# Layer 1's first pass moved ahead of its flag's branch, with chunks loaded or kept under attention and stores issued by GpSimd

## The chip, the cores and the metric

One Trainium2 chip, and of it one core. The time is the device time of one execution in microseconds (us), as the median over runs. A core has five engines that work at the same time, each with its own queue in program order: PE (TensorE, matmuls; its weight loads are listed as PEld), DVE (VectorE), ACT (ScalarE), POOL (GpSimd), and SP (SyncE, which here issues DMA transfers). ACT and POOL can issue DMA transfers too, in queues of their own. Sixteen DMA engines move the data of all queues.

## The reference

Four layers work on x of 256 x 256 x 128 floats, each as x = x + layer(group_norm(x)). The layer that is changed here is the second, called layer 1; layer 0 is the attention whose end comes just before it.

```python
# layer 0: gated triangle attention (4 heads of 32), with pair bias
x = x + _L0_conv_ref(_gn(x), ...)
# layer 1: gated triangle product over 16 channels
def _L1_conv_ref(x, Wa1, ba1, Wa2, ba2, Wb1, bb1, Wb2, bb2, ln2_g, ln2_b, Wg, bg, Wz, bz):
    a = jax.nn.sigmoid((x @ Wa1 + ba1) * (x @ Wa2 + ba2))
    b = jax.nn.sigmoid((x @ Wb1 + bb1) * (x @ Wb2 + bb2))
    g = jax.nn.sigmoid(x @ Wg + bg)
    z = jnp.einsum('bikc,bkjc->bijc', a, b)
    return g * (_ln(z, ln2_g, ln2_b) @ Wz + bz)
x = x + _L1_conv_ref(_gn(x), ...)
# layers 2 and 3 follow: a triangle product over 128 channels, and a layer of small convolutions
```

`_gn` subtracts mean and divides by deviation over groups of 4 channels, taken over the whole image. So layer 1's weights can be folded only when the statistics of all of x1 (the output of layer 0) are known.

## The kernel before

The image is held channel first: x1T in DRAM is 128 channels (partitions) x 65536 tokens. Layers work through it in chunks of SC = 2048 tokens (32 chunks of 1 MB); attention works in groups of GT = 1024 tokens (64 groups of four rows), so that chunk s is groups 2s and 2s + 1.

*Attention (the loop over j, 0 to 2 NG + 4, NG = 64).* Everything inside stands in an order written by hand (`tc.manual_schedule()`). Step j computes scores and weights for two rows, attends the rows of the step before, and finishes older groups: `gate` multiplies by the gate and sends the reciprocal of the softmax sum through DRAM (rz, rb) by SP, `divide` applies it (POOL; for the last group DVE, L730), `output` adds the projection to x (L740), and `close` takes `bn_stats` (L744) and stores the group to x1T (L747; SP, for the last two groups ACT). At j = 2 NG + 2 DVE aggregates the statistics of all groups but the last (`gn_part`, L181), between the divide and the last output. The attention tiles lie in pools on the right side of SBUF (`att_sb`, tags x, xn, rs, qk, vg; `tri_pool` with tri_raw) and on the left (`p2e`, `p2u`).

*The flag.* When attention is done, 13 slots of one chunk each are made on the left, and SP issues the loads of the first 8 chunks (`load1`, L851). The statistics are merged to mv1, and a flag says whether all are finite (L861 to L866). All engines read the flag (L867) and branch on it (L868): if it is set, `general_attention` does layer 0 again in a slower, safe manner. In the runs here it is not set, and the body is jumped over. Behind the branch come the group norm's factors (`gn_groups`) and the folded weights v1, v2, wgf with their offsets (L887 to L902).

*First pass (L921 to L941, by hand).* For each of the 32 chunks PE makes two products (16 matmuls of 32 columns, L927), ACT adds an offset (L936), DVE multiplies (L937), ACT takes the sigmoid one chunk later (L913), and SP stores the result of 256 KB to abD (L918), one to two chunks later still. On SP the store of a chunk stands behind the load of a later chunk into the slot that was just read. The result tile p3_ab has 12 buffers.

*z stage and second pass.* SP loads a and b of two channels at a time from abD (`load_z`), PE multiplies them, and the normalised z goes to znD. The second pass (L1017 to L1097) goes over the chunks in the list `order`, beginning with the 13 that are still in slots: PE and ACT make the gate, PE the product with z, DVE and POOL add to x, SP stores x2T and reloads a slot four steps after its chunk was done. POOL issues the loads of z (L1024). At the end POOL also issues the first four loads of layer 2 (L1160), and SP three more, into tiles that overlie the slots.

Outside the parts in a hand-written order, the framework chooses the order of instructions on each engine; nothing is moved across a branch. Names in the trace drop the stage prefix's number: p3_ab is `p_ab`, p4_z is `p_z`, the chunks are `x`.

Of the kernel before, what the change touches and what calls it, by code (L numbers as in the profile page):

```python
# [15 lines left out]
P = 128  # L16
N = 256
# [14 lines left out]
def kernel(ctx: ExitStack, tc: tile.TileContext, a: dict, out: bass.AP):  # L32
# [162 lines left out]
    def gn_groups(mv, name):  # L195

        with tc.tile_pool(name=name + "_ps", bufs=1, space=PSUM, reuse_waits="tile") as ps, tc.tile_pool(name=name + "_sb", bufs=1, reuse_waits="tile") as sb:
# [4 lines left out]
            d = sb.tile([P, 1], F32, name=name + "_d")  # L202
# [4 lines left out]
            sd = sb.tile([P, 1], F32, name=name + "_sd")  # L207
# [37 lines left out]
    raw = tri_pool.tile([P, NH + 2, 2, N], F32, name="tri_raw")  # L245
# [351 lines left out]

    stats1 = new_stats("stats1")
    rzD = dram.tile([N // 4, 16, N], F32, name="rzD")
    NG = N // G  # L600
    with tc.tile_pool(name="p2e", bufs=6, reuse_waits="tile") as eb, tc.tile_pool(name="p2c", bufs=1, reuse_waits="tile") as cs:
        with att_scope, tc.tile_pool(name="p2u", bufs=2, reuse_waits="tile") as sb, tc.tile_pool(name="p2S", bufs=2, space=PSUM, reuse_waits="tile") as psS, tc.tile_pool(name="p2z", bufs=1, space=PSUM, reuse_waits="tile") as psZ, tc.tile_pool(name="p2M", bufs=3, space=PSUM, reuse_waits="tile") as psM, ExitStack() as by_hand:
            rows = {}
# [119 lines left out]
            def divide(g):  # L723
                t = groups[g]
                if g == NG - 1:

                    rb = psS.tile([P, 2, 2, N], F32, name="p2_S")
                    for r in range(G):
                        nc.tensor.matmul(rb[:, r // 2, r % 2, :], lhsT=pick[:, r, :], rhs=t["rz"], start=True, stop=True)
                    nc.vector.tensor_tensor(t["u"], t["u"], rb.rearrange("p a b n -> p (a b n)"), ALU.mult)  # L730
                    return
# [10 lines left out]
            def close(g, c):  # L742
                x1 = groups[g]["x"]
                nc.vector.bn_stats(stats1[:, g * 2 + c, :], x1[:, c * CK : (c + 1) * CK])  # L744
                if c == 1:
                    queue = nc.sync if g < NG - 2 else nc.scalar
                    queue.dma_start(x1T[:, g * GT : (g + 1) * GT], x1)  # L747
                    del groups[g]
# [21 lines left out]
            for j in range(2 * NG + 5):  # L770
# [5 lines left out]
                if not 0 <= out[0] < NG:  # L776
                    out = None
                if j == 20:
# [34 lines left out]
                if back:  # L813
                    attend(2 * j - 4)
                    gate(2 * j - 4)
                if now:
# [17 lines left out]
                if j == 2 * NG + 2:  # L834
                    mv_first = gn_part(stats1, 0, 2 * NG - 2, "gn1_a")
# [7 lines left out]
    order1 = [b + h * NSC // 2 for b in range(NSC // 2) for h in range(2)]  # L843
    SLOTS, FIRST = 13, 8
    x1_scope = ExitStack()
    slots = [x1_scope.enter_context(tc.tile_pool(name=f"x1_{i}", bufs=1, reuse_waits="tile")) for i in range(SLOTS)]
    xs = {}

    def load1(s, slot):
        xs[s] = slots[slot].tile([P, SC], F32, name="x1", tag="x1")  # L850
        nc.sync.dma_start(xs[s], x1T[:, s * SC : (s + 1) * SC])  # L851

    for i in range(FIRST):
        load1(order1[i], i)


    mv1 = gn_merge(mv_first, gn_part(stats1, 2 * NG - 2, 2 * NG, "gn1_b"), 1.0 - 1.0 / NG, "gn1_mv")
    flag = const.tile([P, 1], mybir.dt.int32, name="flag")
    with tc.tile_pool(name="chk", bufs=1, reuse_waits="tile") as sb, tc.tile_pool(name="chkps", bufs=1, space=PSUM, reuse_waits="tile") as ps:
        ok = sb.tile([P, 2], F32, name="chk_ok")  # L860
        nc.vector.tensor_scalar(ok, mv1, 0.0, 0.0, ALU.mult, ALU.is_equal)  # L861
        pn = ps.tile([P, 2], F32, name="chk_n")
        nc.tensor.matmul(pn, lhsT=ones, rhs=ok, start=True, stop=True)
        bad = sb.tile([P, 2], F32, name="chk_bad")
        nc.vector.tensor_scalar(bad, pn, P - 0.5, None, ALU.is_lt)
        nc.vector.tensor_tensor(flag, bad[:, 0:1], bad[:, 1:2], ALU.max)  # L866
    again = nc.values_load(flag[0:1, 0:1], min_val=0, max_val=1)  # L867
    with tc.If(again > 0):  # L868
        general_attention(
            tc, dict(xT=xT, rsD=rsD, mbD=mbD, triD=triD, x1T=x1T),  # L870
            dict(wf=wf, wo=wo, b_g=b_g, b_o=b_o, cqkg=cqkg, cv=cv, mneg=mneg, ident=ident),
            dram, stats1,
        )
        nc.vector.bn_aggr(mv1, stats1.rearrange("p n s -> p (n s)"))
        for s in order1[:FIRST]:
            nc.sync.dma_start(xs[s], x1T[:, s * SC : (s + 1) * SC])

    m1, r1 = gn_groups(mv1, "gn1")
# [6 lines left out]
    with tc.tile_pool(name="f1ps", bufs=1, space=PSUM, reuse_waits="tile") as ps:  # L889
        for w, wf_, ub, vb, n in ((u1, v1, ub1, vb1, "1"), (u2, v2, ub2, vb2, "2")):  # L890
            nc.vector.tensor_scalar(wf_, w, r1, None, ALU.mult)
            pb = ps.tile([P, 1], F32, name="f1_u" + n)
            for q in range(4):
                nc.tensor.matmul(pb[32 * q : 32 * q + 32, :], lhsT=wf_, rhs=m1, start=True, stop=True)
            nc.vector.tensor_tensor(vb, ub, pb, ALU.subtract)
        nc.vector.tensor_scalar(wgf, wg1, r1, None, ALU.mult)
        pb = ps.tile([P, 1], F32, name="f1_g")
        nc.tensor.matmul(pb, lhsT=wgf, rhs=m1, start=True, stop=True)
        nc.vector.tensor_tensor(bgf, bg1, pb, ALU.subtract)

    c1neg = const.tile([P, 1], F32, name="c1neg")
    nc.vector.tensor_scalar(c1neg, mv1[:, 0:1], -1.0, None, ALU.mult)  # L902
# [1113 lines left out]
```

## Time and profile before

| | us |
|---|---|
| median of 3 runs (lowest, highest) | 3257.12 (3255.87, 3260.84) |
| the profiled execution's own time | 3257.65 |
| its span, first to last instruction | 3255.9 |
| PE busy | 3049.4 |
| DVE busy | 2265.3 |
| ACT busy | 2030.4 |
| POOL busy | 1722.0 |
| attention's last scores to first matmul of the first pass | 1442.25 to 1480.44 |
| first pass, first matmul to last sigmoid's start | 1480.44 to 1555.57 |
| first transpose of the z stage | 1565.71 |
| second pass, first product with z to last chunk's store issued | 1632.62 to 1790.73 |

The granted TensorE clock was 0.971 on average. Times in the text count from the start of the span of this one execution. In a line of instructions a bracket or a last column says how long the engine stood idle before, and what ended it ("<-").

### The profile page before, as it was taken

Reading aid. Unit: us, or ns where it says so; the run is one execution under the profiler, and the core shown is the slowest. Engines: PE = TensorE matmul, PEld = TensorE weight load, DVE = VectorE, ACT = ScalarE, POOL = GpSimd, SP = SyncE. Lnnn points to the kernel's source line nnn. Section 1 sums busy time; section 2 is a strip of 40 time slices with the busy share of each in tenths; the row PEclk is TensorE's granted clock in tenths of the full one; section 3 lists DMA queues with packets and bytes.
Section 4 is the critical chain, followed back from the end, with each engine's and each line's share of the span. In section 5 each row is a group of like instructions: output and inputs, shape, how many; then the busy total and the mean of one; then the engine's idle time right before and its main releaser. Section 6 shows DMA issues by size and latency. Waiting matters only on the chain. (4 is left out here: it accounts for less than half of the span.)

```text
span 3255.9 us, 51705 instructions
## 1 busy us (share of the span) xinstructions
PE 3049.4 (94%) x19908; PEld 1631.7 (50%) x19908; DVE 2265.3 (70%) x2623; ACT 2030.4 (62%) x2272; POOL 1722.0 (53%) x917
## 2 busy tenths in 40 slices
PE   5699999999999999987798899999999989969998
PEld 4535555555555555542533344444699933324444
DVE  5657888888888888883456455455455588858887
ACT  3577777777777777754477544444344457757776
POOL 4006777777777777760277000000255568848787
PEclk8899999999999999998999899999999999989999
DMA  9972333333333333349789577676799989976775
GB/s 376 394 297 95 117 119 107 115 119 108 114 120 109 113 119 110 113 146 398 220 307 412 213 295 300 235 272 247 274 352 351 338 326 388 387 273 196 234 231 154
DMA packets 291508, 748.27 MB, mean 230 GB/s; under 512 B 68473, under 2 KB 139019, under 8 KB 242459
## 3 DMA queue, kind: packets, MB, share of 16 engines
q1 hardware_dynamic: 282065, 731.02, 62.6%
q0 software_dynamic: 6064, 12.21, 1.1%
q8 instruction: 160, 2.62, 0.3%
q10 hardware_dynamic: 3128, 1.67, 0.2%
q14 instruction: 91, 0.75, 0.1%
HBM read 457.35 MB, written 287.45 MB: 229 GB/s over the span
## 5 line engine op out<-in xcount | busy, mean ns | idle before, releaser
L670 POOL TENSOR_TENSOR p_es<-p_e 128x1024 f32<-128x1024 f32 x256 | 603.5, 2368 | 319.4 <-DMA p_x<-xT 196.2
L660 DVE TENSOR_TENSOR p_e<-p_S,tri_raw 128x1024 f32<-128x1024 f32 x512 | 609.6, 1212 | 144.8 <-PE p_S L650 144.7
L668 ACT ACTIVATE p_e<-p_e,mbT 128x1024 f32<-128x1024 f32 x512 | 552.3, 1139 | 61.7 <-DVE p_e L660 61.6
L1221 PE MATMUL p_pm<-p_zn,wf 128*128 128x512 f32 x1040 | 449.2, 593 | 2.2 <-ACT p_a L1256 1.9
L635 PE MATMUL p_mm<-p_xn,w 128*128 128x512 f32 x764 | 404.4, 612 | 0.1
L1221 PEld LDWEIGHTS p_pm<-p_zn,wf 128*128 128x128 f32 x1040 | 196.7, 190 | 254.7 <-issue 246.3
L650 PE MATMUL p_S<-p_qk 32*128 32x256 f32 x4096 | 296.0, 401 | 3.2 <-DVE p_e L660 3.2
L1318 POOL MEMSET k<- 128x512 f32 x1 | 0.5, 524 | 522.9 <-PE p_pm L1221 522.9
L650 PEld LDWEIGHTS p_S<-p_qk 32*128 32x128 f32 x4096 | 186.3, 184 | 159.1 <-PE p_mm L626 91.7
L1974 PE MATMUL tp_z<-p_B,tp_at 128*128 128x256 f32 x1024 | 250.1, 387 | 1.6 <-DMA p_B<-bD 1.4
L683 PE MATMUL p_o<-p_e,p_vg 128*32 128x256 f32 x4096 | 248.3, 383 | 0.0
L617 POOL TENSOR_TENSOR p_xn<-p_xn,p_rs 128x1024 f32<-128x1024 f32 x62 | 148.6, 2396 | 181.1 <-DMA p_rb<-rzD 102.3
L1349 POOL TENSOR_TENSOR k<-k,p_sq 128x512 f32<-128x512 f32 x128 | 162.9, 1272 | 135.9 <-ACT p_sq L1347 135.9
L1974 PEld LDWEIGHTS tp_z<-p_B,tp_at 128*128 128x128 f32 x1024 | 185.2, 191 | 23.6 <-DVE tp_at L1965 2.2
L635 PEld LDWEIGHTS p_mm<-p_xn,w 128*128 128x128 f32 x764 | 125.3, 191 | 104.1 <-issue 88.2
L1348 DVE TENSOR_TENSOR k<-tp_z,k 128x512 f32<-128x512 f32 x128 | 88.6, 692 | 127.4 <-ACT p_sq L1347 127.4
L683 PEld LDWEIGHTS p_o<-p_e,p_vg 128*32 128x32 f32 x4096 | 120.2, 110 | 110.1 <-ACT p_vg L641 41.5
L641 ACT ACTIVATE p_vg<-p_mm,bgh 128x512 f32<-128x512 f32 x128 | 87.9, 687 | 135.0 <-PE p_mm L635 135.0
L1345 ACT COPY p_K<-tp_z 128x512 f32<-128x512 f32 x128 | 74.9, 585 | 154.7 <-PE tp_z L1974 154.7
L1260 DVE SCALAR_TENSOR_TENSOR p_b<-p_pm,b2w,p_b 128x1024 f32<-128x1024 f32 x64 | 82.2, 1284 | 122.7 <-PE p_pm L1221 108.3
L626 PEld LDWEIGHTS p_mm<-w,p_xn 128*128 128x128 f32 x1016 | 133.4, 192 | 61.0 <-issue 60.3
L639 ACT ACTIVATE p_qk<-p_mm,cqkg 128x512 f32<-128x512 f32 x127 | 87.2, 687 | 122.1 <-PE p_mm L635 121.9
(393 smaller groups left out, 6066.8 us busy)
## 6 DMA issues: line engine op xcount, KB each, us to landing
p_x<-x2T SPq DMA_DIRECT2D x60, 1024.0 KB
x<-x1T SPq DMA_DIRECT2D x51, 1024.0 KB
p_x<-in_x_dram SPq DMA_DIRECT2D x32, 1024.0 KB
p_x<-xT SPq DMA_DIRECT2D x64, 512.0 KB
p_rs<-rsD SPq DMA_DIRECT2D x64, 512.0 KB
x2T<-x SPq DMA_DIRECT2D x32, 1024.0 KB
aD<-p_a SPq DMA_DIRECT2D x32, 1024.0 KB
bD<-p_b SPq DMA_DIRECT2D x32, 1024.0 KB
```

What stands on the lines that cost most here:

```text
L617: nc.gpsimd.tensor_tensor(xn, xn, groups[g]["rs"], ALU.mult)
L626: nc.tensor.matmul(pm[:, k * D : (k + 1) * D], lhsT=t["xn"][:, b * P : (b + 1) * P], rhs=wf[:, 2 * D : 3 * D], start=True, stop=True,)
L635: nc.tensor.matmul(pm, lhsT=w, rhs=t["xn"][:, cs_], start=True, stop=True)
L650: nc.tensor.matmul(Ss[h // 2][:, h % 2, u, :], lhsT=t["k"][hp, r * N + u * P : r * N + (u + 1) * P], rhs=t["q"][hp, r * N : (r + 1) * N], ...
L660: nc.vector.tensor_tensor(e[:, :, 2 * p : 2 * p + 2, :].rearrange("p u h n -> p h u n"), Ss[p], triT[:, 2 * p : 2 * p + 2, :, :], ALU.add,)
L668: nc.scalar.activation(e[:, u, :, :], e[:, u, :, :], AF.Exp, bias=mbT[:, u, i : i + 1])
L670: nc.gpsimd.tensor_tensor(es, e[:, 0, :, :], e[:, 1, :, :], ALU.add)
L683: nc.tensor.matmul(t["o"][hp, r % 2, :], lhsT=t["v"][:, r * 2 + u, hp], rhs=e[:, u, h, :], start=(u == 0), stop=(u == 1),)
L1221: nc.tensor.matmul(pm[:, c, :], lhsT=wf2[:, i, :], rhs=zns[s][:, k * CK : (k + 1) * CK], start=True, stop=True)
L1348: nc.vector.tensor_tensor(k1, pz, k1, ALU.add)
L1349: nc.gpsimd.tensor_tensor(k2, k2, sq, ALU.add)
L1974: nc.tensor.matmul(pz[:, t, :], lhsT=at[:, u, t * P : (t + 1) * P], rhs=Bc[:, u, :], start=(u == 0), stop=(u == 1))
```

## The change

- First pass in one piece before the branch. The factors and weights (`weights1`) come right after the statistics; the flag is computed, but read and branched on only after the last chunk's store has been issued. If the branch is taken, layer 0, the weights, the whole first pass and the 13 resident chunks are done again inside it.
- `order1` begins with chunks 14, 15, 0, 16, 1, 17, 30, 31. The first six are loaded during attention by SP (`fill1`) into attention's own tiles, as these come free: chunk 15 at j = 2 NG - 3, chunks 14, 0 and 16 at j = 2 NG - 2, chunks 1 and 17 at j = 2 NG. Chunks 30 and 31 are the last four groups' x tiles, which are kept.
- Twenty slots instead of 13: ten on the left (`near`), loaded after attention, and ten on the right (`far`), on attention's tiles, loaded as the first eight chunks have been read. The last four chunks go to near slots. Seven of the far slots are closed after the pass, so that the second pass has 13 as before, in another order of chunks (`order4`).
- The 31 first stores of abD are issued by POOL, right after their sigmoid, and the last by SP; p3_ab has 5 buffers instead of 12, p3_s1 two instead of three.
- The statistics are aggregated in three parts: the first half at j = 2 NG - 20, most of the rest at j = 2 NG + 1, the last four groups' halves at the end. The last group's divide is done in two halves. ACT touches Sqrt and Sigmoid once ahead of their use. B of the first two z channels is loaded by ACT instead of SP.

The core of the diff (left out: the same attention code, the body of `weights1`, which is the old code in a function, and the branch's body):

```diff
+    order1 = [14, 15, 0, 16, 1, 17, 30, 31] + [b + h * NSC // 2 for b in range(2, NSC // 2 - 2) for h in range(2)]
+    xs = {}
+
+    def fill1(s, x):
+        xs[s] = x
+        for at, xh in spans(x):
+            at += s * SC
+            nc.sync.dma_start(xh, x1T[:, at : at + xh.shape[-1]])
...
-                    nc.vector.tensor_tensor(t["u"], t["u"], rb.rearrange("p a b n -> p (a b n)"), ALU.mult)
+                    for c in range(2):
+                        uc = t["u"][:, c * CK : (c + 1) * CK]
+                        nc.vector.tensor_tensor(uc, uc, rb[:, c].rearrange("p b n -> p (b n)"), ALU.mult)
...
-                    del groups[g]
+                    kept[g] = groups.pop(g)["x"]
...
+                if j == 2 * NG - 2:
+                    fill1(14, tuple(gt_tile(f"x1_14_{h}", "xn", 2) for h in range(2)))
+                    for s, tag, bufs in ((0, "qk", 2), (16, "vg", 3)):
+                        x = att_sb.tile([P, 2, GT], F32, name=f"x1_{s}", tag=tag, bufs=bufs)
+                        fill1(s, x.rearrange("p a t -> p (a t)"))
+                if j == 2 * NG:
+                    fill1(1, tri_pool.tile([P, SC], F32, name="x1_1", tag="tri_raw"))
+                    x = att_sb.tile([P, 2, GT], F32, name="x1_17", tag="qk", bufs=2)
+                    fill1(17, x.rearrange("p a t -> p (a t)"))
...
+                if j == 2 * NG - 20:
+                    mv_early = gn_part(stats1, 0, NG, "gn1_a")
+                if j == 2 * NG + 1:
+                    nc.scalar.activation(const.tile([P, 1], F32, name="root_a"), epst, AF.Sqrt)
+                    mv_first = gn_merge(
+                        mv_early, gn_part(stats1, NG, 2 * NG - 4, "gn1_b"), NG / (2.0 * NG - 4.0), "gn1_c"
+                    )
...
-                if j == 2 * NG + 2:
-                    mv_first = gn_part(stats1, 0, 2 * NG - 2, "gn1_a")
+                if j == 2 * NG - 3:
+                    fill1(15, (gt_tile("x1_15_0", "x", X_BUFS), gt_tile("x1_15_1", "rs", 1)))
...
-    order1 = [b + h * NSC // 2 for b in range(NSC // 2) for h in range(2)]
-    SLOTS, FIRST = 13, 8
...
+    NEAR, FAR, FIRST = 10, 10, 8
+    SLOTS = 13
+    x1_scope, far_scope = ExitStack(), ExitStack()
+    near = [
+        x1_scope.enter_context(tc.tile_pool(name=f"x1_{i}", bufs=1, reuse_waits="tile")) for i in range(NEAR)
+    ]
+    home = {}
+
+    def load1(s, place):
+        home[s] = place
+        xs[s] = place.tile([P, SC], F32, name="x1", tag="x1")
         nc.sync.dma_start(xs[s], x1T[:, s * SC : (s + 1) * SC])
 
-    for i in range(FIRST):
-        load1(order1[i], i)
-
-
-    mv1 = gn_merge(mv_first, gn_part(stats1, 2 * NG - 2, 2 * NG, "gn1_b"), 1.0 - 1.0 / NG, "gn1_mv")
-    flag = const.tile([P, 1], mybir.dt.int32, name="flag")
-    with tc.tile_pool(name="chk", bufs=1, reuse_waits="tile") as sb, tc.tile_pool(name="chkps", bufs=1, space=PSUM, reuse_waits="tile") as ps:
-        ok = sb.tile([P, 2], F32, name="chk_ok")
-        nc.vector.tensor_scalar(ok, mv1, 0.0, 0.0, ALU.mult, ALU.is_equal)
-        pn = ps.tile([P, 2], F32, name="chk_n")
-        nc.tensor.matmul(pn, lhsT=ones, rhs=ok, start=True, stop=True)
-        bad = sb.tile([P, 2], F32, name="chk_bad")
-        nc.vector.tensor_scalar(bad, pn, P - 0.5, None, ALU.is_lt)
-        nc.vector.tensor_tensor(flag, bad[:, 0:1], bad[:, 1:2], ALU.max)
-    again = nc.values_load(flag[0:1, 0:1], min_val=0, max_val=1)
-    with tc.If(again > 0):
-        general_attention(
-            tc, dict(xT=xT, rsD=rsD, mbD=mbD, triD=triD, x1T=x1T),
-            dict(wf=wf, wo=wo, b_g=b_g, b_o=b_o, cqkg=cqkg, cv=cv, mneg=mneg, ident=ident),
-            dram, stats1,
-        )
-        nc.vector.bn_aggr(mv1, stats1.rearrange("p n s -> p (n s)"))
-        for s in order1[:FIRST]:
-            nc.sync.dma_start(xs[s], x1T[:, s * SC : (s + 1) * SC])
-
-
-
-
-
-    m1, r1 = gn_groups(mv1, "gn1")
+    for i, k in enumerate((3, 4, 5, 0, 1, 2, 6, 7, 8, 9)):
+        load1(order1[FIRST + i], near[k])
+    for s, g in ((30, NG - 4), (31, NG - 2)):
+        xs[s] = kept[g], kept[g + 1]
+
+
+    mv1 = gn_merge(mv_first, gn_part(stats1, 2 * NG - 4, 2 * NG, "gn1_e"), 1.0 - 2.0 / NG, "gn1_mv")
...
+    weights1("gn1")
+    nc.scalar.activation(const.tile([P, 1], F32, name="sigmoid_a"), epst, AF.Sigmoid)
+    flag = const.tile([P, 1], mybir.dt.int32, name="flag")
+    chk = const.tile([P, 4], F32, name="chk")
+    with tc.tile_pool(name="chkps", bufs=1, space=PSUM, reuse_waits="tile") as ps:
+        ok, bad = chk[:, 0:2], chk[:, 2:4]
+        nc.vector.tensor_scalar(ok, mv1, 0.0, 0.0, ALU.mult, ALU.is_equal)
+        pn = ps.tile([P, 2], F32, name="chk_n")
+        nc.tensor.matmul(pn, lhsT=ones, rhs=ok, start=True, stop=True)
+        nc.vector.tensor_scalar(bad, pn, P - 0.5, None, ALU.is_lt)
+        nc.vector.tensor_tensor(flag, bad[:, 0:1], bad[:, 1:2], ALU.max)
...
+    after = [16, 17, 14, 15, 22, 23, 28, 29, 30, 31, 12, 13, 24, 25, 2, 3, 4, 5, 8, 9, 10, 11, 0, 6, 1, 7, 18, 19, 20, 21, 26, 27]
+    order4 = [order1[i] for i in after]
+
+    with x1_scope, far_scope:
+        def piece_ab(s, sb, ps):
+            p1 = ps.tile([P, CK], F32, name="p3_1")
+            p2 = ps.tile([P, CK], F32, name="p3_2")
+            for pp, w in ((p1, v1), (p2, v2)):
+                for c in range(4):
+                    nc.tensor.matmul(
+                        pp[32 * c : 32 * c + 32, :], lhsT=w, rhs=piece(xs[s], c), start=True, stop=True
+                    )
+            s1 = sb.tile([P, CK], F32, name="p3_s1", bufs=2)
+            nc.scalar.activation(s1, p1, AF.Identity, bias=vb1)
+            nc.vector.scalar_tensor_tensor(s1, p2, vb2, s1, ALU.add, ALU.mult)
+            return s1, sb.tile([P, CK], F32, name="p3_ab", bufs=5)
+
+        with tc.tile_pool(name="p3", bufs=2, reuse_waits="tile") as sb, tc.tile_pool(name="p3ps", bufs=3, space=PSUM, reuse_waits="tile") as ps, tc.manual_schedule():
+            open_ab = []
+
+            def close3(queue):
+                s, s1, ab = open_ab.pop(0)
                 nc.scalar.activation(ab, s1, AF.Sigmoid)
+                queue.dma_start(abD[:, s * CK : (s + 1) * CK], ab)
+
             for i, s in enumerate(order1):
+                if i == FIRST:
+                    att_scope.close()
+                    far = [
+                        far_scope.enter_context(tc.tile_pool(name=f"x1_r{k}", bufs=1, side="right", reuse_waits="tile"))
+                        for k in range(3)
+                    ]
+                    over_scope = ExitStack()
+                    far += [
+                        over_scope.enter_context(tc.tile_pool(name=f"x1_r{k}", bufs=1, side="right", reuse_waits="tile"))
+                        for k in range(3, FAR)
+                    ]
+                    for m, k in enumerate((9, 4, 3, 8, 1, 0, 2, 7, 6, 5)):
+                        load1(order1[FIRST + NEAR + m], far[k])
+                open_ab.append((s, *piece_ab(s, sb, ps)))
+                if i + NEAR + FAR < NSC and i >= FIRST:
+                    load1(order1[i + NEAR + FAR], home[s])
                 if i:
+                    close3(nc.gpsimd)
+            close3(nc.sync)
+        over_scope.close()
+
+        again = nc.values_load(flag[0:1, 0:1], min_val=0, max_val=1)
+        with tc.If(again > 0):
...
-                        nc.sync.dma_start(
+                        (nc.sync if g else nc.scalar).dma_start(
                             B[:, c, :], abD.rearrange("(q c) (s t) -> c s q t", q=4, t=CK)[16 + 2 * g + c]
...
-            order = [order1[i] for i in (*range(20, NSC), 19, 18, *range(18))]
+            order = order4
...
-                    load1(order[j], (j + 7) % SLOTS)
+                    load1(order[j], home[order[j - SLOTS]])
```

## The prediction

> **What bounds the kernel now.** I read the page's engine shares first, then each engine's busy time by stretch around the edited lines, then SP's waits, the groups of the first pass, and the timeline at the branch. The page gives PE 3049.4 us of 3255.9 (94%); what PE lacks lies largely between 1447 and 1640 us, from attention's end over layer 1's first pass (L921 to L941) into the z stage. Columns below: stretch, its length, busy us (instructions) of PE, PEld, DVE, ACT, POOL, then granted clock, DMA share, GB/s.
>
> ```profile
> 1440.00:1450.00 10.00, 10.00 (x144) 4.95 (x140) 8.42 (x10) 4.38 (x4) 4.57 (x3) 0.98 0.20 61
> ...
> 1455.00:1460.00 5.00, 4.48 (x12) 2.35 (x10) 3.37 (x5) 0.00 (x0) 0.00 (x0) 0.76 1.01 428
> ...
> 1470.00:1475.00 5.00, 0.00 (x0) 0.00 (x0) 0.00 (x0) 1.28 (x1) 0.00 (x0) 0.50 0.94 381
> 1475.00:1480.00 5.00, 1.71 (x21) 1.51 (x21) 1.74 (x10) 0.26 (x1) 0.00 (x0) 0.50 0.48 143
> ...
> 1490.00:1500.00 10.00, 10.00 (x100) 2.76 (x92) 4.25 (x6) 7.06 (x13) 0.00 (x0) 1.00 1.02 424
> ...
> 1530.00:1540.00 10.00, 6.50 (x60) 1.61 (x52) 2.25 (x3) 4.36 (x8) 0.00 (x0) 1.00 1.02 421
> ...
> 1560.00:1565.00 5.00, 0.00 (x0) 0.00 (x0) 0.00 (x0) 0.00 (x0) 0.00 (x0) 0.50 0.39 118
> ```
>
> The DMA engines are full from 1450 to 1560 at some 424 GB/s, except around 1475 to 1480, where they are half empty; during attention they are nearly free (0.20). PE runs full only until about 1519.
>
> ```profile
> L927 PE MATMUL p<-x,v 128*32 128x512 f32 x512 | 59.5, 612 | 12.7 <-DMA x<-x1T 12.7
> L913 ACT ACTIVATE p_ab<-p_s 128x512 f32<-128x512 f32 x32 | 20.0, 626 | 25.3 <-DMA abD<-p_ab 25.0 <-DVE p_s L937 0.3
> L181 DVE BATCH_NORM_AGGREGATE gn_a<-stats 128x2 f32<-128x756 f32 x1 | 3.6, 3559 | 0.0
> ```
>
> PE waits 12.7 us for chunks and ACT 25.0 us for its stores to free a buffer, although it has 12: the stores stand in SP's queue behind the chunk loads, as SP's waits show.
>
> ```profile
> SPq L918 <- DMA x<-x1T: 11.6, 6, 2.1
> SPq L867 <- DVE flag L866: 11.4, 1, 11.4
> ...
> SPq L868 <- SPq L868: 6.0, 2, 3.6
> ```
>
> ```profile
> 1469.16 0.16 DVE L866 TENSOR_TENSOR flag<-chk_bad 128x1 int32<-128x1 f32 x1
> ...
> 1476.09 0.15 DVE L902 TENSOR_SCALAR c1neg<-gn_mv 128x1 f32<-128x1 f32 x1 [6.78 <-DVEq L868]
> ...
> 1476.84 3.31 SPq L851 DMA_DIRECT2D x<-x1T  x5
> ```
>
> From the flag to DVE's next work are 6.8 us, and SP, which issued 8 loads ahead of the branch, issues the other 5 only at 1476.84. So the first pass is bound by bytes: 32 loads (33.6 MB), 32 stores (8.4), and three late x1T stores (1.6) are 43.6 MB, at 424 GB/s 103 us; with the gap of 5.5 us, from 1451 to 1559.5, as seen. The first transpose of z starts at 1565.7, after loads issued at 1561.68.
>
> **The change, part by part.**
>
> *Bytes.* Chunks 30 and 31 stay in attention's tiles: two loads fewer. Chunk 15 (issued at j = 125, about 1429), and 14, 0, 16 (j = 126, about 1433) come while DMA stands at 0.14 to 0.20: 4.2 MB, 10 us. Chunks 1 and 17 follow at j = 128, once bias L660 has left tri_raw (1447). After about 1449.5 remain 26 loads (27.3 MB), 1.6 and 8.4: 37.2 MB, 88 us, so nothing lands last before 1537.5. Ten near slots and ten far ones keep loads queued; the far ones need chunks that PE finishes by about 1487, when the near loads (done about 1481) have just been followed by the first of them.
>
> *SP's queue.* Eight more DMA issues of about 0.33 us (L851) are moved into attention, 2.6 us of SP. They wait for PE and POOL releases of j = 125 and 126. Queued behind are the x1T store of j = 126 and group 62's rz and rb of j = 127 (1444.18 to 1448.2), which POOL's divide at 1451.77 needs. About 10 us separate them, so I cost this at nothing; without that cover each us of lateness moves attention's end by one.
>
> *Statistics.* Half of bn_aggr goes to j = 108. L181 costs 3.559 us for 756 elements and 0.209 for 12, 4.5 ns an element: 384 cost 1.9 us, in a place where PE is full and DVE idle some 15%. Bounds 0 and 1.9 us; I take +1. The other part (1.8 us and the merge, 1 us) comes at j = 129, where DVE waits 1.96 us for PE; the 3.56 us ahead of the last L740 go, the halved L730 gives 0.6. mv1 comes about 2 us sooner, at 1466. The preloaded tables replace 1.28 us on ACT that lay beside the branch, or beside PE's first chunk.
>
> *Start of the pass.* The weights' chain took 4.0 us (1476.44 to 1480.44); the check's matmul on PE adds up to 1. PE starts about 1471 instead of 1480.4. This is worth nothing by itself while bytes are the bound. PE needs 59.5 us (L927), so 1530.5 at the earliest.
>
> *Stores by GpSimd.* 31 issues of 0.6 us on a POOL that is idle (0.00 above). They leave SP's order, and share the engines with the loads. The nearest row:
>
> ```profile
> p_z<-znD POOLq DMA_DIRECT2D x12, 256.0 KB, 11.1
> ```
>
> The same size and 2 KB runs, issued in pairs under a full DMA: landings 8.8, 11.1, 13.4 us (lowest, median, highest). After some 3 us of start a pair takes about 8, so one store about 4.1 us. Here a rule bears: the Trainium skill's "DMA: Bandwidth & Descriptors", section "Queues, rings and completion order", says that each DMA engine goes round its queues a packet at a time. One store's share against one load's share gives 1.31 MB a turn, 3.1 us per store. It speaks against this change in that a store no longer gets what it needs: PE could close a chunk each 1.72 us. By either pace PE can be ten chunks ahead of the last landed store (five p_ab, two p_s1, three pairs of PSUM).
> The first sigmoid ends about 6.3 us after PE's start (as before), 1477.3; first landing about 1482. By then 12 MB of 28.8 are in. With 3.1 us the rest loads at 339 GB/s, until 1527; about 15 stores landed, PE at chunk 25 or 26, 6.5 left x 1.72 = 11 us, last sigmoid 2.3 later: 1540.5. With 4.1: loads done 1524.5, 11 stores landed, 10.5 chunks left, 18 us, 1545. I take 3.6, the middle: 1543 (before: last store issued 1557.9). By the rule alone the total below would be 2.5 us less, by the row 2 us more. Behind a store that waits for ACT stands nothing on POOL until the z stage's adds (L998).
>
> The same skill's "SBUF — State Buffer", section "Who interferes with whom", warns that DVE's two-port modes lock GpSimd out of writing descriptors. The row: POOL issues of L1024, beside L1075 on DVE, took 592 to 657 ns. By the row 0, by the rule at most one DVE instruction (0.75 us, L937) per store; hidden, as POOL has 1.7 us a chunk. I take 0.
>
> *Branch at the end.* All engines pass it after their last work. SP went from flag to its last L868 event in 7.4 us with DMA full; the last store's landing covers 3.8 us of that (1557.9 to 1561.68). Bounds 3.8 (landing alone) and 7.4; with DMA nearly empty I take 5. The z loads then start at 1548 instead of 1561.7: 13.7 us. Two B loads on ACT (1.2 us of issue) run beside A; the first multiply waited for ACT's copy of A, so 0.
>
> *Second pass.* Same 19 reloads, other order and slots. At its end POOL's adds wait behind layer 2's loads:
>
> ```profile
> POOL p_x L1160 <- DMA x2T<-x: 6.9, 1, 6.9
> ```
>
> By the order of allocation, the slots under GpSimd's four tiles are last used at positions 22 to 24, instead of 19 to 22. If the loads keep their place in POOL's order, the wait grows by up to 3 x 4.7 us; if they move behind the last adds, some 4 us of it go. The trace cannot say; bounds -5 and +10, I take 0.
>
> **Sum.** -13.7 + 1 = -12.7 us. The profiled execution took 3257.65 (span 3255.9 and 1.8 around it), 0.5 over the median of 3257.12: 3245.0, and 3244.4 against the median. I write 3244.5. Within 0.2% (6.5 us, about what a measurement of this kernel tells from no change) means 3250.6 to 3263.6.
>
> **Rivals.**
> *Stores keep up* (0.20): the shares even out, the pass ends by bytes, last sigmoid 1538.5, z at 1543 (-18.5), and POOL's wait at the second pass's end shrinks: 3236 to 3240. For it: 37.2 MB set only 1537.5. Against: the 8.8 to 13.4 us.
> *The gain is given back* (0.13): the branch costs its 7.4 us and POOL's adds wait 7 us longer: about 3252 to 3256. For it: the 6.9 us wait. Against: its place is open. Here belongs, too, that the early loads are not early because SP stands at a release: then 4.2 MB, 10 us, return behind 1449.5.
> *Slower* (0.07): GpSimd's queue, not the sharing, sets the 4.1 us, so 2 KB stores pace the whole pass. Last sigmoid at 1477.3 + 31 x pace; with 5 us of branch it turns against the change above (1556.7 - 1477.3) / 31 = 2.6 us per store, and 4.1 gives 1604, about 3305. Against: a 1 MB load of the same queue (p_x from x3T) lands in 8.1 us, which leaves about 2 us for a quarter of it.
> *The likeliest case* (0.60): 3240 to 3250.
>
> **Numbers.** Faster by over 0.2%: 0.60, 0.20 and a sixth of 0.13: 0.82. Within: the rest, 0.11. Slower: 0.07. The range of 8 in 10 runs from 3236 (stores keep up) to 3253 (half of what is given back); slower is left out.
>
> **What would show it.** Six x loads before 1449.5 and DMA above 0.4 around 1430; first L927-like matmul near 1471; PE without a wait for x, but waits for PSUM behind ACT's wait for its stores after chunk 13 or so; store landings of 7 to 13 us while loads are queued; DMA full to about 1525, then not; z loads at 1548. I am wrong if PE waits for chunks late in the pass, if store landings stay long after the loads are done, or if the second pass takes more than 5 us more or less than its 161 (1632 to 1793).

## The result, and the profile after

The changed kernel took 3238.36 us (median; 3234.86 to 3240.66) beside 3257.32 for the kernel before, both measured together: ratio 0.9937, 95% interval 0.9925 to 0.9949. Measured once more in another group it was 0.9951 (0.9936 to 0.9967). The profiled execution took 3240.66, its span 3238.9. Predicted were 3244.5, in a range of 3236 to 3253; the likeliest case was put at 3240 to 3250, and 3236 to 3240, where the result lies, was the range of the rival "stores keep up".

The part of the program ahead of layer 1, which the change hardly touches, ends at times that differ by several us between executions of any of these kernels (attention's last scores matmul starts at 1443.0 in before's profile, 1446.8 in after's, 1440.2 in the changed kernel's second one). So every stage is counted here from that matmul (L659 after). Counted so, the two profiles of the changed kernel agree within 0.4 us:

| us after attention's last scores matmul | before | after | after, second profile |
|---|---|---|---|
| first product of the first pass | 37.4 | 26.6 | 26.5 |
| start of its last sigmoid | 112.6 | 98.0 | 98.0 |
| first load of z's A | 118.7 | 103.4 | 103.4 |
| first transpose of the z stage | 122.7 | 110.2 | 110.0 |
| first product of the second pass | 189.6 | 176.1 | 175.9 |
| last store of x2T issued | 347.7 | 331.3 | 331.7 |

16.4 us are gained by the end of layer 1. From that store to the end of the span it is 1465.2 us before and 1460.8 after, but this stretch has nearly the same code in all kernels shown here and lies between 1458.0 and 1465.7 us in them; what it adds in one profile is not ascribed to the change.

First the busy times by stretch of the changed kernel (columns as in the prediction):

```profile
1445.00:1450.00 5.00, 5.00 (x76) 2.55 (x70) 4.52 (x5) 1.08 (x2) 2.77 (x2) 1.00 0.26 102
1450.00:1455.00 5.00, 4.30 (x62) 1.76 (x54) 4.10 (x6) 3.67 (x4) 1.78 (x1) 1.00 0.82 247
...
1520.00:1540.00 20.00, 12.11 (x108) 2.87 (x96) 6.00 (x8) 10.96 (x18) 4.87 (x9) 1.00 1.01 420
1540.00:1545.00 5.00, 2.17 (x20) 0.50 (x16) 1.50 (x2) 2.13 (x5) 0.90 (x2) 1.00 0.30 108
```

The DMA engines are full up to about 1541 (1.01 of the time, 420 GB/s in 1520 to 1540), which is to the last chunk, not to 1525 as predicted. Just ahead of it, at attention's end, is a hole: 0.26 in 1445 to 1450.

The groups of the first pass, and the timeline of PE at its end:

```profile
L937 PE MATMUL p<-x,v 128*32 128x512 f32 x480 | 57.0, 619 | 10.5 <-DMA x<-x1T 8.3 <-ACT p_ab L950 1.3 <-ACT p_s L941 0.5
...
L950 ACT ACTIVATE p_ab<-p_s 128x512 f32<-128x512 f32 x32 | 20.1, 628 | 15.6 <-DMA abD<-p_ab 12.8 <-DVE p_s L942 2.8
```

```profile
1534.78 1.92 PE L937 MATMUL p<-x,v 128*32 128x512 f32 x16 [1.62 <-DMA x<-x1T]
1538.32 1.92 PE L937 MATMUL p<-x,v 128*32 128x512 f32 x16 [1.62 <-DMA x<-x1T]
1541.96 1.92 PE L937 MATMUL p<-x,v 128*32 128x512 f32 x16 [1.72 <-DMA x<-x1T]
```

ACT's wait for store buffers has halved (25.0 to 12.8 us) though there are five instead of 12. PE's wait for chunks, 12.7 us before, is still 8.3 us, and it stands at the end: each of the last five chunks is waited for, and one comes every 3.6 us (the last three are shown). That is the sign that the prediction named as proof against itself. What paces a chunk at 3.6 us shows in the queues of a stretch inside the pass (packets, MB, share of the 16 engines) and in the stores' group:

```profile
q1 hardware_dynamic: 1392, 10.16, 68.9%
q0 software_dynamic: 1393, 4.58, 32.3%
...
abD<-p_ab POOLq DMA_DIRECT2D x18, 256.0 KB, 8.9
```

In these 35 us (1500 to 1535) SP's queue q1 with the loads and GpSimd's queue q0 with the stores have the same number of packets, 1392 and 1393 (so they do in the same stretch of e6, 1392 and 1392, and of e11, 1397 and 1396). 18 stores in 35 us are 1.94 us for one, and the loads get what is left, 10.16 MB in 35 us = 290 GB/s, 3.6 us for a chunk.

The end of the pass on the timeline:

```profile
1545.44 0.34 SPq L951 DMA_DIRECT2D abD<-p_ab  x1
...
1550.20 4.49 SPq L1012 DMA_DIRECT2D z_ab<-abD  x8
...
1557.04 1.95 PE L2014 MATMUL tp_a<-ident,z_ab 128*128 128x128 f32 x8 [13.15 <-DMA z_ab<-abD]
```

From the last store's issue to the first load of z it is 4.8 us, with the branch in between; from there to the first transpose 6.8 us, where it was 4.0 before.

GpSimd at the end of the second pass:

```profile
1768.34 0.58 POOL L1211 DMA_DIRECT2D p_x<-x2T  x1
1772.39 4.49 POOL L1137 TENSOR_TENSOR x<-x,p_g 128x2048 f32<-128x2048 f32 x1 [3.46 <-DVE p_g L1126]
1776.83 1.61 POOL L1211 DMA_DIRECT2D p_x<-x2T  x3
```

One load of layer 2 stands ahead of the last add and three behind it; the wait of 6.9 us for a tile is gone.

### The profile page after: what moved, and what is told of

Read it like the earlier page. It is cut to its first block, busy times and chain, and to the rows that moved or that the text cites. A ratio compares the mean times of both kernels' runs of the same rounds, so it can differ in the third digit from the quotient of the medians.

```text
span 3238.9 us, 51714 instructions
## 1 busy us (share of the span) xinstructions
PE 3052.9 (94%) x19908; PEld 1633.7 (50%) x19908; DVE 2263.2 (70%) x2630; ACT 2034.6 (63%) x2274; POOL 1739.0 (54%) x948
## 5 line engine op out<-in xcount | busy, mean ns | idle before, releaser
L659 PE MATMUL p_S<-p_qk 32*128 32x256 f32 x4096 | 295.5, 400 | 3.3 <-DVE p_e L669 3.3
L659 PEld LDWEIGHTS p_S<-p_qk 32*128 32x128 f32 x4096 | 186.0, 184 | 159.2 <-PE p_mm L635 91.7
```

The source lines that it names most:

```text
L659: nc.tensor.matmul(Ss[h // 2][:, h % 2, u, :], lhsT=t["k"][hp, r * N + u * P : r * N + (u + 1) * P], rhs=t["q"][hp, r * N : (r + 1) * N], ...
```

## Experiments

All but e10 are edits of the changed kernel. Ratios are to the kernel before, measured in the same group; times of stages are counted as above, from one profile of each. The groups' runs of the kernel before have medians of 3253.84 (e1 to e4), 3251.84 (e5 to e8) and 3257.52 (e9 to e12). The changed kernel was not run in the third group, so a ratio there stands beside 0.9937 and 0.9951 of the other two.

| | ratio (95% interval) | first product | last sigmoid | z loads | first transpose | second pass: first product | last store |
|---|---|---|---|---|---|---|---|
| after | 0.9937 (0.9925, 0.9949) | 26.6 | 98.0 | 103.4 | 110.2 | 176.1 | 331.3 |
| e1 stores by SP | 0.9992 (0.9984, 1.0001) | 26.5 | 110.9 | 116.0 | 122.4 | 189.7 | 344.6 |
| e2 stores by ACT | 0.9969 (0.9956, 0.9981) | 26.3 | 104.5 | 109.4 | 115.6 | 183.0 | 338.2 |
| e3 three buffers | 0.9964 (0.9950, 0.9978) | 26.6 | 102.3 | 108.0 | 114.9 | 182.4 | 338.1 |
| e4 no branch | 0.9953 (0.9937, 0.9970) | 26.0 | 98.1 | 101.0 | 107.8 | 175.0 | 329.8 |
| e5 after again | 0.9951 (0.9936, 0.9967) | 26.5 | 98.0 | 103.4 | 110.0 | 175.9 | 331.7 |
| e6 late loads (hoisted) | 0.9933 (0.9911, 0.9955) | 29.1 | 95.4 | 100.8 | 107.5 | 172.6 | 328.6 |
| e7 near order | 0.9944 (0.9924, 0.9965) | 26.6 | 97.9 | 103.3 | 109.5 | 175.5 | 330.7 |
| e8 B on SP | 0.9933 (0.9909, 0.9957) | 26.2 | 98.8 | 104.2 | 108.6 | 176.2 | 332.3 |
| e9 late, in order | 0.9982 (0.9974, 0.9990) | 26.4 | 108.5 | 113.9 | 120.1 | 186.5 | 342.8 |
| e10 before, layer 2's loads on SP | 0.9995 (0.9986, 1.0005) | 37.3 | 112.6 | 118.7 | 122.8 | 190.4 | 345.1 |
| e11 z loads ahead | 0.9970 (0.9961, 0.9980) | 26.2 | 98.0 | 101.4 | 113.2 | 179.9 | 334.5 |
| e12 z ahead, chunk 17 by ACT | 0.9961 (0.9946, 0.9976) | 28.5 | 97.5 | 101.0 | 112.5 | 178.3 | 335.1 |

### e1: the stores back on SP

```diff
-                    close3(nc.gpsimd)
+                    close3(nc.sync)
```

> All 32 stores of the first pass are issued by SP again, with five p_ab buffers and everything else as in the changed kernel. Theory (a queue of their own is what lets the stores through): on SP the ten far loads stand behind store 6, which waits for its sigmoid, so DMA has a hole, and store 7 stands behind ten far loads (10.5 MB, 25 us). ACT then waits for p_ab around chunk 12. Last sigmoid about 11 us later than in the changed kernel, time 3249 (3244 to 3257). Rival (the bytes decide, whatever the queue): last sigmoid within 2 us, time 3237 to 3240. My prediction's step of 3.6 us per store on GpSimd's queue would make the gap smaller than 11 us.

The theory holds: last sigmoid 12.9 us later than in the changed kernel, and nearly all the gain is gone (0.9992). ACT on the timeline, between chunks 11 and 12:

```profile
1491.02 0.62 ACT L950 ACTIVATE p_ab<-p_s 128x512 f32<-128x512 f32 x1
1517.18 0.63 ACT L950 ACTIVATE p_ab<-p_s 128x512 f32<-128x512 f32 x1 [24.34 <-DMA abD<-p_ab]
```

A single wait of 24.3 us is the time of ten chunk loads in front of one store in the same queue. The PE time is lost there, and the DMA share falls to 0.68 in 1520 to 1540, when only stores are left.

### e2: the stores on ACT's queue

```diff
-                    close3(nc.gpsimd)
+                    close3(nc.scalar)
```

> The 31 stores are issued by ACT instead of GpSimd. Theory A (any queue of its own will do, the 16 DMA engines share between queues): pace of stores again about 2.0 us, landing about 9 us with five buffers, last sigmoid within 2 us, time 3237 to 3241. Theory B (GpSimd's packets, 4 KB in the trace, win a larger share than those of another queue): pace above 2.5 us while loads run, so that 6 or more chunks are left when the loads are done, last sigmoid 4 to 12 us later, time 3242 to 3250.

The last sigmoid came 6.5 us later, inside what theory B gave. In 1500 to 1535 both queues together moved 13.6 MB (389 GB/s) where the changed kernel moved 14.8 (423 GB/s), and their packets look unequal:

```profile
q1 hardware_dynamic: 1279, 9.30, 68.9%
q10 hardware_dynamic: 2340, 4.27, 31.7%
```

That is a mean over two kinds of stretch. From 1510 to 1520 both queues have work, and from 1502 to 1506 the loads' queue runs low:

```profile
q1 hardware_dynamic: 459, 3.37, 79.9%
q10 hardware_dynamic: 452, 0.83, 21.5%
...
q10 hardware_dynamic: 408, 0.75, 48.7%
q1 hardware_dynamic: 100, 0.69, 50.3%
```

In the first, ACT's and SP's packets alternate one for one too (459 and 452), and 420 GB/s are moved. A packet of these stores is 1.8 KB on average, small ones included, against 3.3 KB on GpSimd's queue. So the stores get 83 GB/s, 3.2 us for one: theory B's pace above 2.5 us, and its reason. (B's next step, chunks left over when the loads are done, did not come: PE waits for the last chunk here too.) In the second, four packets of five are the stores' small ones, and 363 GB/s are moved; just behind it, from 1508 to 1509, it is 82. SP's waits in 1450 to 1550 show what held up the loads:

```profile
SPq L881 <- DMA abD<-p_ab: 30.5, 4, 10.4
```

Ahead of four loads SP waited 30.5 us in all, by this view for stores that ACT had issued; in the changed kernel SP has no such wait at this line. Why a load waits there for a store was not isolated. PE waited 14.4 us for chunks. So a queue of their own, whichever, brings about half of the 12.9 us that e1 lost, and GpSimd's queue the other half. How that half divides between the larger packets and SP's waits is open.

### e3: three store buffers

```diff
-            return s1, sb.tile([P, CK], F32, name="p3_ab", bufs=5)
+            return s1, sb.tile([P, CK], F32, name="p3_ab", bufs=3)
```

> p_ab has three buffers instead of five. Theory A (the landing time is given, and buffers divided by it set the pace, as my prediction assumed): landing stays 8.9 us, pace (8.9 + 1.2) / 3 = 3.4 us, 16 chunks stored when the loads are done, last sigmoid about 15 us later, time about 3253. Theory B (the queue is served at a rate of about 2.0 us a store, 131 GB/s, and the 8.9 us are only the stores waiting behind each other): landing falls to about 5 us, pace stays 2.0 to 2.2 us, last sigmoid within 3 us, time 3237 to 3242.

Neither theory had the size. The queue in 1500 to 1535:

```profile
abD<-p_ab POOLq DMA_DIRECT2D x14, 256.0 KB, 6.4
```

14 stores in 35 us are 2.5 us for one, and GpSimd's queue is not always filled (1103 packets beside 1528 of SP's); landing fell from 8.9 to 6.4 us with fewer stores ahead. 6.4 us and about 1.2 of sigmoid and issue, divided by three, give 2.5: with three buffers the round trip sets the pace. With five, (8.9 + 1.2) / 5 = 2.0 gives the pace too, but now the landing itself is the queue: at 2 us a store, four stores ahead of it are 8 of the 8.9 us. The landing time is a result of the pace there, not its cause. The last sigmoid came 4.3 us later: the loads were done sooner and stores remained.

### e4: without the branch

```diff
-        again = nc.values_load(flag[0:1, 0:1], min_val=0, max_val=1)
-        with tc.If(again > 0):
...
```

> The read of the flag, the branch and its body (the redo of layer 0 and of the pass) are left out; with the flag not set the computation is the same. Theory (branch and code loading are on the path behind the last store): z loads start when the last stores have landed, about 2.2 us after the last store's issue instead of 4.8, and the first transpose comes 3 to 5 us earlier against the last sigmoid, time 3234 to 3235.5. Rival (the landing covers the branch): z loads at the same distance, time unchanged within 1 us.

SP and PE at the end of the pass:

```profile
1540.81 0.32 SPq L951 DMA_DIRECT2D abD<-p_ab  x1
...
1543.13 4.74 SPq L989 DMA_DIRECT2D z_ab<-abD  x8
```

2.3 us instead of 4.8 from the last store to the z loads: 2.4 us of the branch lie on the path behind a store that has landed, as the theory said. The first transpose is 2.4 us earlier (3 to 5 expected), the first product of the second pass 1.1, the last store 1.5. The median of the time is too coarse to show this (0.9953 against 0.9937 and 0.9951 for the kernel with the branch).

### e5: the changed kernel again

> The changed kernel once more, as a control beside the runs of this group. Counted from the start of attention's last scores, in its first profile the first product of the pass came at 26.6 us, the last sigmoid at 98.0, the z loads at 103.4, the first transpose at 110.2, the first product of the second pass at 176.1, its last store at 331.3. The same within 1 us is expected, and a ratio to the kernel before of 0.992 to 0.995.

All stages came within 0.4 us. The ratio is 0.9951, beside 0.9937 in the first group. The two intervals overlap; the 16.4 us of the stages, 0.9950 of 3257, lie inside the second and just outside the first.

### e6 and e9: the early loads issued late

```diff
-        for at, xh in spans(x):
+
+    def late1(s):
+        for at, xh in spans(xs[s]):
...
+    for s in order1[:6]:
+        late1(s)
     for i, k in enumerate((3, 4, 5, 0, 1, 2, 6, 7, 8, 9)):
```

> The six chunks that are loaded under attention are put into the same tiles, but their DMAs are issued after attention, ahead of the near loads. Theory (the pass ends by bytes): 4 MB of the 6 were read before attention's end and now follow it, 4.2 MB at 424 GB/s = 9.9 us; the first product stays at 26.6 us after attention's last scores, the last sigmoid comes 8 to 10 us later (106 to 108 instead of 98.0), time 3246 to 3249. Rival (stores, ACT or PE set the end, as in my prediction's sum): last sigmoid less than 4 us later, PE without waits for x in the last chunks.

The edit did not do what it says: outside the hand-written order the framework hoisted the DMAs into attention. SP in e6:

```profile
1428.78 0.36 SPq L607 DMA_DIRECT2D x<-x1T  x1
...
1447.86 0.36 SPq L607 DMA_DIRECT2D x<-x1T  x1
...
1451.74 0.43 SPq L607 DMA_DIRECT2D x<-x1T  x1
```

So the run tests neither theory. It tells something else: the first product started 2.5 us later than in the changed kernel and the last sigmoid 2.6 us earlier, so that an earlier start of PE is not what sets the end of this pass. One chunk is issued at 2.6 us after the last scores matmul instead of 4.7. The hole of the DMA engines is still there; in the 2.5 us behind the last scores matmul they stand at 0.01 (0.08 in the changed kernel):

```profile
1445.30:1447.80 2.50, 2.50 (x34) 1.00 (x30) 2.50 (x3) 0.00 (x0) 1.79 (x1) 1.00 0.01 3
```

In the stages e6 is the fastest version of all (328.6 at the last store); its median, 3232.49, and the changed kernel's in the same group, 3235.35, lie closer than either interval is wide, so that it is not shown faster.

e9 makes the same edit inside the hand-written order, at j = 2 NG + 1:

```diff
+                if j == 2 * NG + 1:
+                    for s_ in order1[:6]:
+                        late1(s_)
```

> The six early chunks in the same tiles, their DMAs now fixed in the hand-written order, at j = 2 NG + 1, so that they cannot be hoisted as in e6. Theory (the pass ends by bytes): 4.2 MB that were read before attention's end follow it, last sigmoid 106 to 109 us after attention's last scores instead of 98.0, time 8 to 10 us over the changed kernel's. Rival (ACT's waits for store buffers set the end): last sigmoid under 102.

The last sigmoid at 108.5 instead of 98.0, 10.5 us later, beside 9.9 us for 4.2 MB; PE's wait by the view of waits:

```profile
PE p L942 <- DMA x<-x1T: 19.7, 15, 1.7
```

That is 11.4 us more than in the changed kernel, over 15 chunks instead of five. The bytes theory holds, and the early loads are worth about 10 us by the stages (11.5 at the last store).

### e7: the near slots in plain order

```diff
-    for i, k in enumerate((3, 4, 5, 0, 1, 2, 6, 7, 8, 9)):
+    for i, k in enumerate(range(10)):
```

> The near slots are filled in their plain order 0 to 9 instead of 3, 4, 5, 0, 1, 2, 6 to 9; nothing else. First pass unchanged. Theory (the slots' order decides when layer 2's first four tiles come free, and with that whether POOL's loads for them stand ahead of its last adds): three or four of these loads stand ahead of the last add again, POOL waits there, the second pass is 2 to 5 us longer from its first product to its last store (155.2 us in the changed kernel, 158.1 before), time 3240 to 3243. Rival (the shorter second pass has another cause, such as the order of the chunks): within 1 us of 155.2.

The rival: the second pass takes 155.2 us from first product to last store, as in the changed kernel, and GpSimd again has one load ahead of its last add and three behind. The order of the near slots does not place them. The first near load was issued 6.5 us after the last scores matmul instead of 8.8, yet the last sigmoid came only 0.1 us earlier.

### e8: B of the first channels on SP

```diff
-                            (nc.sync if g else nc.scalar).dma_start(
+                            nc.sync.dma_start(
```

> B of the first two z channels is loaded by SP again, behind A of the same channels, instead of by ACT beside it. Theory (B on a second queue takes engines from A, which is needed first, while A of the next channels stands ahead): from the first z load to the first transpose 4 to 4.5 us instead of 6.8, the first product of the second pass 1 to 2.5 us earlier against the z loads, time about 1.5 us less. Rival (engines that fetch code after the branch delay it): 6.8 us as before, time unchanged.

From z loads to first transpose 4.4 us instead of 6.8, as the theory said: B beside A makes A late. But the first product of the second pass comes 72.0 us after the z loads, 72.7 and 72.4 in the two profiles of the changed kernel, and 71.8 and 72.2 in e6 and e7, which have B on ACT: of the 2.4 us nothing is shown to arrive. The medians of this group (3232.19 here, 3235.35 for the changed kernel) do not tell them apart.

### e10: the kernel before, layer 2's first loads off GpSimd

```diff
-                (nc.gpsimd if s < KB else nc.sync).dma_start(xs[s], x2T[:, s * SC : (s + 1) * SC])
+                nc.sync.dma_start(xs[s], x2T[:, s * SC : (s + 1) * SC])
```

> The kernel before, with the first four loads of layer 2 issued by SP instead of POOL; nothing else. Theory (the second pass got shorter because POOL's adds no longer stand behind these loads): POOL's wait of 6.9 us goes, first product to last store of the second pass 154 to 156 us instead of 158.1, time about 3 us less (ratio 0.999). Rival (the other order of chunks and slots made it shorter, or SP, standing at these loads, holds up x2T's stores): 157.5 us or more, ratio 1.000 to 1.002.

The second pass took 154.7 us instead of 158.1. GpSimd's last two adds (in the kernel before, 6.9 us of waiting and three loads stand among its last three adds):

```profile
1770.04 4.53 POOL L1086 TENSOR_TENSOR x<-x,p_g 128x2048 f32<-128x2048 f32 x1 [0.17 <-DVE p_g L1075]
1778.54 4.51 POOL L1086 TENSOR_TENSOR x<-x,p_g 128x2048 f32<-128x2048 f32 x1 [3.97 <-DVE p_g L1075]
```

They wait for DVE alone now. So the 2.9 us by which the second pass is shorter in the changed kernel are the size of what these loads cost ahead of the adds. From e1 to e9, whose edits do not touch the second pass, its length lies between 154.8 and 156.3 us, so that each of these differences is known to about 1 us. The ratio, 0.9995 (0.9986 to 1.0005), neither shows nor excludes 3 us.

### e11 and e12: z loads ahead of the branch

```diff
+        for g in range(2):
+            load_z(g)
+
         again = nc.values_load(flag[0:1, 0:1], min_val=0, max_val=1)
...
+            for g in range(2):
+                fetch_ab(g)
```

Left out are the pools: the tiles of these loads get pools of their own, made ahead of the branch.

> The loads of the first two pairs of z channels are issued ahead of the flag's read and branch, and once more in the branch's body. Theory (the branch is on the path of the z loads): z loads at 101 us after attention's last scores instead of 103.4, the first transpose 2.5 to 5 us earlier (105 to 107.5), the first product of the second pass 1.5 to 3 us earlier (173 to 174.5), time 2 us less than the changed kernel. Rival (PE and ACT, which pass the branch later because ACT waits for the last store first, set the first transpose): first transpose at 109 or later, no gain.

The z loads do start at 101.4, but the first transpose comes at 113.2, 3 us later than in the changed kernel. PE and SP:

```profile
1551.55 1.24 SPq L990 DMA_DIRECT2D z_ab<-abD  x2
1557.38 1.95 PE L2028 MATMUL tp_a<-ident,z_ab 128*128 128x128 f32 x8 [16.07 <-SPq L1004]
```

PE is released by SP's branch (L1004). SP issues ten loads first (ACT the other two), up to 1552.8, then branches, and 4.6 us later PE begins. The rival said "no gain", and it is a loss: the last to reach the branch is SP, not ACT.

e12 adds to this:

```diff
-                    fill1(17, x.rearrange("p a t -> p (a t)"))
+                    fill1(17, x.rearrange("p a t -> p (a t)"), nc.scalar)
...
-                        (nc.sync if g else nc.scalar).dma_start(
...
+                (nc.sync).dma_start(
```

> As e11, with B of the first pair on SP, and chunk 17 loaded by ACT at the start of j = 2 NG, when its tile is free but SP still stands at the reciprocals (e6 had this chunk 3.6 us earlier by accident, and its last sigmoid came at 95.4). Theory (bytes and branch both count): last sigmoid 95 to 96.5, z loads 98.5 to 100, first product of the second pass 170 to 172.5, time 4 to 6 us less than the changed kernel, ratio to the kernel before 0.991 to 0.994. Rival (the early chunk only moves the hole in DMA): last sigmoid 97.5 or later, gain as in e11.

The branch costs the same here (first transpose at 112.5). The early chunk 17 brought 0.5 us (97.5), not 2: the rival's side, and the ratio, 0.9961, stayed outside the 0.991 to 0.994 of the theory. The near loads that follow began at 8.8 us as before. So why e6 gained 2.6 us, and e7 and e12 hardly anything with a chunk that is just as early, is left open.

## Why the prediction was right, and where not

**The bytes after attention** (26 chunk loads, nothing lands last before 1537.5). This step carried the result. The last chunk came at 1541.96; less the 3.8 us by which attention ended later in this profile, that is 1538.2. e9 prices the step: giving the 4.2 MB back costs 10.5 us. Its condition is that the stores get through beside the loads: e1, with the same bytes and the stores on SP, ends the pass 12.9 us later.

**The pace of the stores** (3.1 to 4.1 us, taken 3.6). This is the term that was mis-sized. It measured 1.94 us. With 3.6 the loads would have been done at 1524 to 1527, with chunks left to the stores; in fact the stores kept up and the loads ended last, as in the rival "stores keep up". Two errors are in the term. The upper end came from dividing the landing time of stores behind each other, which is a property of how many are queued (e3: 8.9 and 6.4 us for five and three buffers). The lower end applied the rule of one packet per queue and turn to packets of the wrong size, the 2 KB of a row. The trace has 1392 and 1393 packets for the two queues, and 4.58 MB / 1393 = 3.3 KB for a packet of q0 against 7.3 KB for one of q1, small ones included. One for one, these sizes give the stores 31% of 423 GB/s, which is 131 GB/s, 2.0 us for one. So the rule was right, and the size of GpSimd's packets was wrong; the Trainium skill's "DMA: Bandwidth & Descriptors", section "SWDGE vs HWDGE vs iDMA", also says that a packet is up to 4096 bytes preferably, and that would have given the size. For ACT's queue, whose packets are 1.8 KB on average, the 3.1 us of the prediction come out nearly as they stand: 3.2 us in e2, where both queues have work.

**The last sigmoid** (1543, 12.6 us earlier). 14.6 us earlier. The rival's 1538.5 and the 3.8 us of attention make 1542.3; it started at 1544.8. Most of the remaining 2.5 us lies behind the last chunk: that chunk came 0.7 us later than the bytes allowed (1538.2 beside 1537.5), and from its first product to the last sigmoid it is 2.8 us (1541.96 to 1544.79), for which the rival left 1.0. The hole in the DMA at attention's end is a loss that the prediction did not count, but what it costs is not shown: e6 has it too and ends 2.6 us earlier.

**Statistics and PE's start** (1471; one more us under attention). 10.8 us earlier relative to attention's end, 9.4 predicted. It was rightly costed as no gain by itself: e6 starts 2.5 us later and ends earlier. From first to last scores matmul it is 1199.1 us before and 1199.3 and 1196.0 in the two profiles after, so the 1 us for the aggregation under attention was not needed.

**The branch** (5 us from last store to z loads, 3.8 to 7.4). 4.8 us; e4 shows that 2.4 of them are the branch itself, the rest is the store's landing. The gain of moving it, 1561.7 to 1548, was taken as 13.7 us; 15.3 came.

**DVE's lock** (0). GpSimd's issue of a store took 540 ns, at most 571, beside DVE's work: the row was right, and nothing of the warning is seen.

**B on ACT** (0). Wrong at the first transpose, where it costs 2.4 us (e8); at the second pass no cost is shown. The argument that the first multiply waits for ACT's copy anyway overlooked that A itself comes later when B runs beside it.

**The second pass's end** (-5 to +10, taken 0). -2.9 us, by the case that was named in it: the loads have moved behind the last adds. e10 shows 3.4 us for that in the kernel before. What in the change moved them stays open; e7 excludes the order in which the near slots are filled.

**The sum.** -13.7 us at the z loads were -15.3; on the way to the second pass 1.8 us were given back (-13.5), about 1 us of which may be spread between profiles (from the z loads on it is 70.9 us in the kernel before and 71.8 in e10, with the same code there); the second pass added -2.9: -16.4 at its end, where -12.7 was written. The median of the first group lies 2.6 us lower still, that of the second where the stages have it (-16.5). The number was right in part by luck: the end of the first pass went by the case that was given a chance of 0.20, not by the sum's own, and the result is inside the range because the range was drawn out to take that case in. At the end of layer 1 the sum was off by 3.7 us: 2.0 at the last sigmoid, 2.9 in the second pass and 1.0 for the aggregation under attention, less 0.4 at the branch and the 1.8 that were given back.

## What to carry to other kernels

In a pass that is full of DMA, first count the bytes that are left when it begins: they set its end here as long as stores had a queue beside the loads and buffers enough, and an engine's earlier start was not what set it (e6). A store that shares a queue with ten prefetches waits for all of them. The landing time of a transfer in a backlog is queue length times pace, so take the pace from packets or bytes, not from the landing. And count packets in a stretch where both queues have work: the mean over a longer one hides a queue that runs low (e2).

## What the runs showed of the hardware that was not expected

- A store issued by GpSimd goes in larger packets than the same store issued by ACT (3.3 against 1.8 KB on average over 35 us). Beside a full queue of loads a store then takes 1.94 us on GpSimd's queue and 3.2 us on ACT's.
- GpSimd's queue and SP's alternated packet by packet (1393 and 1392), and so did ACT's and SP's while both had work (452 and 459 in e2). With the stores on ACT's queue SP's loads stood still for 30.5 us in all, by the view of waits for these stores; with the stores on GpSimd's no load waited for one.
- Jumping over a body that is not executed costs far more than an instruction: 4.6 us from SP's last load to PE's first matmul in e11, where PE and DVE are both released by SP's branch. The changed kernel has nine packets of the two instruction queues between 1540 and 1552 us, against four between 1500 and 1535, and e4, without the branch, has one in the stretch that corresponds (1535.3 to 1547.3); the Trainium skill's "Runtime: NRT & Kernel Launch", section "Instruction fetch mechanics", says that a branch to a target outside the loaded window has to fetch code first, which would fit. No run here separates fetching from meeting.
- Not of the chip but of the framework: DMAs outside a hand-written order were issued up to 33 us ahead of the last scores matmul although they stand behind attention in the program (e6).
